# Two state-space layers on a 64x64 image: another load of x, a convolution shared three to one, and a table load moved behind two copies

## The chip, the cores and the metric

The kernel runs on one core of one Trainium2 chip. The metric is the device time of one execution in microseconds; the median of three runs stands for the kernel. The profile is of one further execution, with its own time. In the text, PE or TensorE is the matrix engine, DVE is VectorE, ACT is ScalarE, POOL is GpSimd, and SP is the engine that issues most of the transfers.

## What is computed

The input x is an image of 64x64 positions with 96 channels. Two layers of the same kind are applied, each added to its own input:

```python
x = x + _L0_conv_ref(_gn(x), ...)
x = x + _L1_conv_ref(_gn(x), ...)
```

`_gn` normalises the 96 channels in 32 groups of three, over all positions of a group. A layer then is, cut to what matters:

```python
xz = x @ in_proj_w                      # 96 -> 2 * 192
x_val, z = xz[..., :192], xz[..., 192:]
xc = conv3x3_depthwise(x_val) + conv_b
u = silu(xc)
y = sum of four selective scans over u  # rows and columns, both ways, 16 states each
y = layernorm(y) * ln_g + ln_b
y = y * silu(z)
return y @ out_proj_w
```

Layer 0 and layer 1 differ in the form of the scan and in the orders in which the positions are visited.

## The kernel before

**Layout.** Channels lie on partitions and the 4096 positions along the free axis. `xT` holds the 96 channels of x, 96x4096. The 192 inner channels are kept as three blocks b = 0, 1, 2 of 64 channels. A block has 128 partitions: partitions 0 to 63 hold its channels for one half of the positions and 64 to 127 those of the other half. Each half has four chunks c of 512 positions (eight image rows); `NCH` is 4 and `HT` 512. `u`, `y` are such blocks of 128x2048.

**Constants and the load of x** (lines 84 to 163). ScalarE loads the table for exponential and logarithm, VectorE and GpSimd build an identity, selectors and other constants, and `gav` (the matrix that averages groups of three channels, line 120) is read. Then x is read in eight pieces of 512 positions, alternately from the SP queue and the ScalarE queue, into tiles `xt` of which four exist. A partition receives four separate positions of 96 floats, 384 B each (line 158). TensorE transposes each piece in four products into a PSUM tile `pt`, and VectorE copies that into `xT` (line 163). At the end of the program text, but before the layers, VectorE takes `bn_stats` of each piece of `xT` (line 1347), and `xT` is stored to a buffer `xs` in DRAM (line 1348), from which the end of the layer reads it back.

**A layer.** The weights are read on the SP queue (lines 1353 to 1359 and `scan_weights`, lines 189 to 215); `ds` is a small sum over weights on VectorE (line 1361). Then come `head`, the scans, and `tail`.

**`head`** (from line 1123). Zero borders are set on three padded images `pad`. `bn_aggr` (line 1141) joins the statistics; two small products with `gav` give the mean `gm` and the variance of each group, and ScalarE makes `rs`, one over the deviation, from a logarithm and an exponential (lines 1150 and 1151). VectorE normalises `xT` into `xn` in eight pieces (line 1156). `project(b, c)` multiplies with the input weights and ScalarE copies the result into `pad` (lines 1163 and 1167); `borders(b)` computes the neighbouring rows once more for the chunk edges (lines 1181 and 1185). Then the 3x3 convolution runs in two forms:

- `conv(b, s)` on VectorE, two chunks at a time: nine taps on shifted views, one scaling (line 1237) and eight multiply-and-adds into `acc` (line 1239), of which three buffers exist.
- `conv_by_products(b, c)` on TensorE, one chunk: nine products with diagonal matrices `diag` (lines 1216 and 1251). A product in fp32 shows as two entries in the profile.

VectorE does blocks 0 and 1, TensorE block 2. `finish` (line 1206) applies Silu on ScalarE into `u`, and starts `y` as u times `ds` (line 1121). `gate(b, c)` projects z on TensorE (line 1193), applies Silu on ScalarE into `sz`, of which three buffers exist (line 1198), and stores that to `szd` (line 1199), twelve times.

**Scans.** Layer 0 runs `near_scans` (from line 246), a short form in which only states near the ends of the sequence matter, with a test; the full form `far_scans` runs only if the test fails. Layer 1 runs `scans` (from line 654), in eight groups of a direction and a chunk. There every instruction is kept behind the one before it on its engine in program text, with a list of due slots for the preparation of later groups. All its instructions show line 668, a helper. `first` prepares the first group: projections `pj` of the last chunk of all three blocks, their copies `xd`, the products `pd` and from them, per block, Abs, exponential and logarithms on ScalarE. ScalarE's table for exponential and logarithm is loaded ahead of all that; the head has used the table of Silu.

**What sets the order.** Outside `scans` a scheduler orders the instructions of each engine when the program is built: among instructions that it takes as ready it picks the one that stands first in the program text. Each engine then follows its own fixed order and waits at each instruction for its inputs and buffers. The memory of the load's tiles is used again by the head, and that of the head by the scans, so that the later part waits for the earlier one's last readers.

Of the kernel before, what the change touches and what calls it, by code (L numbers as in the profile page):

```python
# [8 lines left out]
F32 = mybir.dt.float32  # L9
BF16 = mybir.dt.bfloat16  # L10
AF = mybir.ActivationFunctionType
ALU = mybir.AluOpType
# [4 lines left out]
HW = 64  # L17
L = HW * HW
DM = 96
# [5 lines left out]
HT = TC // 2  # L25
NCH = L // TC
SR = HT // HW
# [16 lines left out]
def two_ss2d_layers(  # L44
# [41 lines left out]
    def load_exp_ln():  # L86
        table("natural_log_exp_and_others")
# [3 lines left out]
    ident = const.tile([128, 128], F32, name="ident")  # L91
# [25 lines left out]
    eps5 = const.tile([128, 1], F32, name="eps5")  # L117
    nc.vector.memset(eps5, 1e-5)
    gav = const.tile([DM, DM], F32, name="gav")
    nc.sync.dma_start(out=gav, in_=gavg)  # L120

# [25 lines left out]
    xs = dpool.tile([DM, L], F32, name="xs")  # L147
# [2 lines left out]

    xp = ExitStack()
    xT = xp.enter_context(tc.tile_pool(name="xT0", bufs=1)).tile([DM, L], F32, name="xT0")
    with tc.tile_pool(name="ld", bufs=4) as ld, tc.tile_pool(
        name="ldp", bufs=4, space=PSUM
    ) as ldp:
        xr = x.rearrange("(g j p) c -> g p j c", p=128, j=4)
        for g in range(8):
            xt = ld.tile([128, 4, DM], F32, tag="xt", name=f"xt{g}")
            (nc.sync if g % 2 == 0 else nc.scalar).dma_start(out=xt, in_=xr[g])
            pt = ldp.tile([DM, 512], F32, tag="pt", name=f"pt{g}")  # L160
            for j in range(4):
                nc.tensor.transpose(pt[:, j * 128 : (j + 1) * 128], xt[:, j, :], ident)
            nc.vector.tensor_copy(xT[:, g * 512 : (g + 1) * 512], pt)

    def columns(t, h, cols):

# [487 lines left out]
    def scans(weights):  # L654
# [4 lines left out]
        xw, dwb, _ = weights  # L659
# [13 lines left out]
        with ExitStack() as sc:  # L673
# [1 line left out]
            mn = sc.enter_context(tc.tile_pool(name="mn", bufs=3))  # L675
            pps = sc.enter_context(tc.tile_pool(name="pps", bufs=1, space=PSUM))
            dram = sc.enter_context(tc.tile_pool(name="dram", bufs=3, space=DRAM))
            load_exp_ln()
            am = []
            carry = pre.tile([128, 3, NP], F32, name="carry")  # L680
            PER = 3 * NP
# [234 lines left out]
            def first(  # L916
                project, projected, rows, delta, spread, tokens_B, tokens_B_out,
                first_part, less_part, next_part, tokens_du, tokens_du_out,
            ):
                parts = [delta(T) for T in range(3)]  # L920
                for h in range(2):
                    project(h)
                for h in range(2):
                    projected(h)
                rows()
                for begin, by_scalar, by_vector in parts:
                    begin()
                tokens_B()
                for T, (begin, by_scalar, by_vector) in enumerate(parts):
                    by_scalar()  # L930
                    if T == 1:
                        tokens_B_out()
                        am.extend(decays(weights[2]))
                    by_vector()
                    spread(T)
                    if T < 2:
                        fetch_c(0, T)
                stage_a(0)
                for h in range(2):
                    first_part(h)  # L940
                for h in range(2):
                    less_part(h)
                for h in range(2):
                    next_part(0, h)
                for h in range(2):
                    less_part(h)
                for e in range(4):
                    tokens_du(e)
                for e in (0, 2, 1, 3):
                    tokens_du_out(e)  # L950
                for h in range(2):
# [171 lines left out]
    def head(l, xT, w):  # L1123

        ipw_s, v, ds = w["ipw"], w["v"], w["ds"]
        with ExitStack() as sc:
            cv = sc.enter_context(tc.tile_pool(name=f"cv{l}", bufs=1))
            cw = sc.enter_context(tc.tile_pool(name=f"cw{l}", bufs=3))
# [7 lines left out]
                nc.gpsimd.memset(t[HALF[1], NCH - 1, SR + 1, 1 : HW + 1], 0.0)  # L1136


            gst = cv.tile([DM, 6], F32, name=f"gst{l}")
            gm, rs = gst[:, 2:3], gst[:, 5:6]  # L1140
            nc.vector.bn_aggr(gst[:, 0:2], w["st"].rearrange("p a b -> p (a b)"))
            pm = cvp.tile([DM, 1], F32, tag="z", name=f"pm{l}", bufs=3)
            nc.tensor.matmul(pm, gav, gst[:, 0:1], start=True, stop=True)
# [6 lines left out]
            nc.scalar.activation(rs, pv, AF.Ln, bias=eps5[0:DM])  # L1150
            nc.scalar.activation(rs, rs, AF.Exp, scale=-0.5)

            xn = cv.tile([DM, L], F32, name=f"xn{l}")
            for g in range(8):
                s = slice(g * 512, (g + 1) * 512)
                nc.vector.tensor_scalar(xn[:, s], xT[:, s], gm, rs, ALU.subtract, ALU.mult)
            xr = xn.rearrange("p (r w) -> p r w", w=HW)

            def project(b, c):
# [43 lines left out]
            W2 = HW + 2  # L1203

            def finish(b, cut, of):
                nc.scalar.activation(
                    u[b][:, cut].rearrange("p (c r w) -> p c r w", r=SR, w=HW), of, AF.Silu,
                    bias=v[:, b, V_CB : V_CB + 1],
                )
                start_y(nc.scalar.mul, ds, b, cut)  # L1210
# [14 lines left out]
            def conv(b, s):  # L1225


                room = cw.tile([128, 2, SR, W2], F32, tag="acc", name=f"acc{l}_{b}_{s}")
                acc = room.rearrange("p c r w -> p c (r w)")[:, :, 0 : SR * W2 - 2]
                for k, (i, j) in enumerate(taps):  # L1230
                    o = i * W2 + j
                    src = pad[b].rearrange("p c r w -> p c (r w)")[
                        :, 2 * s : 2 * s + 2, o : o + SR * W2 - 2
                    ]
                    wk = v[:, b, V_CW + k : V_CW + k + 1]
                    if k == 0:
                        nc.vector.tensor_scalar_mul(acc, src, wk)
                    else:
                        nc.vector.scalar_tensor_tensor(acc, src, wk, acc, ALU.mult, ALU.add)  # L1239
                finish(b, slice(1024 * s, 1024 * (s + 1)), room[:, :, :, 0:HW])  # L1240

            for b in (0, 1, 2):
                project(b, 0)
# [5 lines left out]
            diag = cv.tile([128, len(taps), 128], F32, name=f"diag{l}")  # L1249
            for k in range(len(taps)):  # L1250
                nc.scalar.mul(diag[:, k, :], ident, v[:, 2, V_CW + k : V_CW + k + 1])
            conv(0, 0)
            for c in range(NCH):
                conv_by_products(2, c)
            for b, s in ((1, 0), (0, 1), (1, 1)):
                conv(b, s)
            for b in range(3):
                for c in range(NCH):
                    gate(b, c)
# [82 lines left out]
                    if 0 <= i - lag < NCH:  # L1342
                        step(order[i - lag])

    st = [pers.tile([DM, 8, 6], F32, name=f"st{l}") for l in range(2)]
    for g in range(8):
        nc.vector.bn_stats(st[0][:, g, :], xT[:, g * 512 : (g + 1) * 512])
    nc.sync.dma_start(out=xs, in_=xT)
    for l in range(2):

        w = {"st": st[l], "next": st[1]}
# [16 lines left out]
        else:  # L1368
# [6 lines left out]
        xT = xp.enter_context(tc.tile_pool(name=f"xT{l + 1}", bufs=1)).tile(  # L1375
            [DM, L], F32, name=f"xT{l + 1}"
        )
# [81 lines left out]
```

## Time and profile before

| what | value |
|---|---|
| median of three runs | 1553.86 us (1553.56 to 1554.03) |
| profiled execution, its own time | 1545.96 us |
| its span in the profile | 1543.8 us |
| load of x and statistics, to the start of `xn` in layer 0 | 0 to 23.61 us |
| head of layer 0, to the first product of `near_scans` | 23.61 to 89.05 us |
| `near_scans` and the tail of layer 0, to the start of `xn` in layer 1 | 89.05 to 225.63 us |
| head of layer 1, to the first projection of `scans` | 225.63 to 289.95 us |
| granted TensorE clock, whole span | 0.913 of full speed |

In a line of a timeline the columns are: start in us from the start of the span, length in us, engine, line of the kernel, operation, output and input by the names of the tiles, shape, count of instructions that the line merges, and in brackets how long the engine stood idle before it and what released it. A line that merges several instructions gives the time from the first start to the last end. PEld is the loading of weights into TensorE; a name with q (SPq, ACTq) is an engine's queue, where transfers are issued. In the chain that ended last the columns are start, length and what the time was spent in.

### The profile page before, as it was taken

The numbers are of one execution on the slowest core, as the hardware profiler recorded it, in microseconds if no ns is written. First come the engines' busy times: TensorE is split into PE (matmuls) and PEld (weight loads), VectorE is DVE, ScalarE is ACT, GpSimd is POOL, SyncE is SP. The second block draws the span as 40 slices with busy tenths as digits, with TensorE's granted clock in tenths as the row PEclk, the third lists the DMA queues.
The fourth block names the chain that finished last, engine by engine and source line by source line (L and its number), as shares of the span: only waits on it lengthen the run. The fifth ranks groups of instructions, "written<-read, shape, count | busy, mean of one in ns | idle before, by whom it ended". The sixth has DMA issues, their size and how long they took to land.

```text
span 1543.8 us, 17370 instructions
## 1 busy us (share of the span) xinstructions
PE 1258.3 (82%) x5158; PEld 507.0 (33%) x5158; DVE 1354.3 (88%) x942; ACT 1196.7 (78%) x2459; POOL 1102.9 (71%) x593
## 2 busy tenths in 40 slices
PE   5953779798897888798888889797979888877778
PEld 3432424233332323232323333333333332322223
DVE  6936389469999999999999999999999999999976
ACT  3456125669989898898999999999898989897733
POOL 0032100149898999899898989898989899998860
PEclk8975689869999999998999999999999899999999
DMA  4031330441625344352626162526263544526223
GB/s 111 11 107 45 89 87 1 127 106 37 144 74 133 82 111 108 85 126 68 151 55 153 55 138 57 137 57 146 65 140 76 124 97 96 123 70 146 74 81 96
DMA packets 82674, 146.32 MB, mean 95 GB/s; under 512 B 31580, under 2 KB 33820, under 8 KB 82476
## 3 DMA queue, kind: packets, MB, share of 16 engines
q1 hardware_dynamic: 79884, 142.78, 38.2%
q0 software_dynamic: 576, 1.57, 0.4%
q10 hardware_dynamic: 2112, 0.79, 0.2%
q8 instruction: 42, 0.69, 0.2%
q14 instruction: 60, 0.49, 0.1%
HBM read 80.85 MB, written 12.13 MB: 60 GB/s over the span
## 4 chain that ended last, share of the span: by engine, by line
DVE 26%; issue 21%; PE 13%; ACT 11%; POOL 7%; DMA 6%; SPq 5%; DVEq 0%; POOLq 0%; ACTq 0%
DVE h L668 17%; DVE b L668 6%; POOL hc L668 5%; SPq L668 5%; ACT a L668 4%; PE ys L668 3%; ACT bT L668 2%; PE pj L668 2%; PE b L668 2%; PE cp L1216 2%; DMA cb<-C 2%; DMA du<-su 2%; DMA xT<-xs 1%; PE pd L668 1%; PE in L1163 1%
## 5 line engine op out<-in xcount | busy, mean ns | idle before, releaser
L668 POOL TENSOR_TENSOR hc<-h,cb 128x1024 f32<-128x1024 f32 x384 | 902.7, 2367 | 116.3 <-DVE h L668 61.8
L668 DVE TENSOR_TENSOR_SCAN h<-a,carry,b 128x1024 f32<-128x1024 f32 x288 | 665.2, 2337 | 30.3 <-PE b L668 6.4
L668 ACT ACTIVATE a<-dt,am 128x1024 f32<-128x1024 f32 x384 | 438.6, 1142 | 94.3 <-DVE h L668 91.3
L668 PE MATMUL ys<-hc,fold 128*64 128x512 f32 x1536 | 434.2, 645 | 2.6 <-POOL hc L668 2.6
L668 ACT ACTIVATE bT<-duT,BT 128x192 f32<-128x192 f32 x1012 | 387.2, 445 | 8.3 <-PE b L668 6.4
L668 PE MATMUL b<-ident,bT 128*128 128x128 f32 x1536 | 223.5, 289 | 34.3 <-DVE h L668 27.4
L668 DVE TENSOR_TENSOR b<-b,du 128x1024 f32<-128x1024 f32 x192 | 232.2, 1209 | 12.3 <-PE b L668 12.3
L668 PEld LDWEIGHTS b<-ident,bT 128*128 128x128 f32 x1536 | 176.6, 147 | 160.9 <-DVE h L668 99.1
L668 DVE TENSOR_TENSOR_SCAN h<-a,b 128x1024 f32<-128x1024 f32 x96 | 216.1, 2278 | 13.9 <-PE b L668 6.0
L668 PE MATMUL b<-B,selh 96*128 96x512 bf16 x384 | 122.4, 402 | 90.0 <-DVE h L668 89.9
L668 PEld LDWEIGHTS ys<-hc,fold 128*64 128x64 f32 x1536 | 79.0, 140 | 142.2 <-issue 102.8
L668 PEld LDWEIGHTS <-selh 96*128 96x128 bf16 x384 | 25.9, 98 | 220.9 <-DVE h L668 124.1
L668 PE MATMUL pj<-u,xw 64*124 64x512 f32 x192 | 94.2, 636 | 3.1 <-ACT sz L1198 1.7
L668 PE MATMUL pd<-xd,dwb 29*64 29x512 f32 x192 | 58.2, 677 | 47.0 <-DVE w L668 40.1
L1239 DVE SCALAR_TENSOR_TENSOR acc<-pad,v,acc 128x1052 f32<-128x1052 f32 x64 | 79.6, 1308 | 0.2
L668 POOL DMA_DIRECT2D du<-su x12 | 6.4, 538 | 81.7 <-ACT am L226 79.7
L668 PE MATMUL ys<-y,ident 128*128 128x512 f32 (+1 forms) x120 | 64.7, 646 | 0.0
L1216 PE MATMUL cp<-pad,diag 128*128 128x512 f32 x144 | 62.3, 593 | 0.0
L668 ACT CAST B<-pj 96x512 bf16<-96x512 f32 (+2 forms) x96 | 54.9, 575 | 4.5 <-PE pj L668 4.5
L668 POOL TENSOR_TENSOR sp<-sp,ln 128x512 f32<-128x512 f32 x45 | 57.4, 1275 | 0.2
L668 POOL TENSOR_TENSOR ln<-ln,w 128x512 f32<-128x512 f32 x45 | 57.4, 1276 | 0.0
L668 POOL TENSOR_TENSOR su<-sp,u 128x512 f32<-128x512 f32 x45 | 57.3, 1274 | 0.0
(173 smaller groups left out, 1173.7 us busy)
## 6 DMA issues: line engine op xcount, KB each, us to landing
cb<-C SPq DMA_DIRECT2D x256, 256.0 KB, 4.1
dt<-sp SPq DMA_DIRECT2D x192, 128.0 KB, 4.2
du<-su SPq DMA_DIRECT2D x180, 128.0 KB, 4.2
szd<-sz SPq DMA_DIRECT2D x24, 256.0 KB, 3.1
szt<-szd SPq DMA_DIRECT2D x24, 256.0 KB, 6.8
xT<-xs SPq DMA_DIRECT2D x8, 384.0 KB
xs<-xT SPq DMA_DIRECT2D x1, 1536.0 KB
xs<-xT SPq DMA_DIRECT2D x8, 192.0 KB, 2.3
```

The costliest lines, as they stand in the source:

```text
L668: return lambda *args, **more: tc.keep_in_program_order(op(*args, **more))
L1163: nc.tensor.matmul(ps[half], ipw_s[:, 64 * b : 64 * b + 64], xn[:, g * 512 : (g + 1) * 512], start=True, stop=True,)
L1216: nc.tensor.matmul(ps.rearrange("p (r w) -> p r w", w=HW), diag[:, k, :], pad[b][:, c, i : i + SR, j : j + HW], start=(k == 0), stop=(k == ...
L1239: nc.vector.scalar_tensor_tensor(acc, src, wk, acc, ALU.mult, ALU.add)
```

## The change

Six edits are made:

1. The load of x. A partition now receives four consecutive positions, 1536 B in one piece. All eight transfers are issued ahead of the transposes, into eight buffers. The copy from PSUM into `xT` is made by ScalarE and puts the positions in order, so that it writes every fourth element in turn. The statistics are taken by VectorE from PSUM, in the same loop.
2. The store of `xT` to `xs` and the read of `gav` stand at the end of the load, in this order; `st` is allocated ahead of it.
3. Normalisation: every second piece of `xn` is made by ScalarE as an Identity with scale `rs` and bias `shift`, which VectorE computes beforehand as minus mean times `rs`.
4. TensorE convolves chunks 0 to 2 of block 2; chunk 3 is convolved by VectorE, as the last of its convolutions. `conv` takes a range of chunks.
5. `load_exp_ln()` of `scans` stands behind the two copies `projected` of the first group, and no longer at the start.
6. In `gst` a seventh column holds `shift`.

```diff
-    nc.sync.dma_start(out=gav, in_=gavg)
...
-    with tc.tile_pool(name="ld", bufs=4) as ld, tc.tile_pool(
+    st = [pers.tile([DM, 8, 6], F32, name=f"st{l}") for l in range(2)]
+    with tc.tile_pool(name="ld", bufs=8) as ld, tc.tile_pool(
         name="ldp", bufs=4, space=PSUM
     ) as ldp:
-        xr = x.rearrange("(g j p) c -> g p j c", p=128, j=4)
+        xr = x.rearrange("(g p j) c -> g p j c", p=128, j=4)
+        xts = [ld.tile([128, 4, DM], F32, tag="xt", name=f"xt{g}") for g in range(8)]
         for g in range(8):
-            xt = ld.tile([128, 4, DM], F32, tag="xt", name=f"xt{g}")
-            (nc.sync if g % 2 == 0 else nc.scalar).dma_start(out=xt, in_=xr[g])
-            pt = ldp.tile([DM, 512], F32, tag="pt", name=f"pt{g}")
+            (nc.sync if g % 2 == 0 else nc.scalar).dma_start(out=xts[g], in_=xr[g])
+        for g in range(8):
+            pt = ldp.tile([DM, 4, 128], F32, tag="pt", name=f"pt{g}")
             for j in range(4):
-                nc.tensor.transpose(pt[:, j * 128 : (j + 1) * 128], xt[:, j, :], ident)
-            nc.vector.tensor_copy(xT[:, g * 512 : (g + 1) * 512], pt)
+                nc.tensor.transpose(pt[:, j], xts[g][:, j, :], ident)
+            nc.scalar.copy(
+                xT[:, g * 512 : (g + 1) * 512].rearrange("c (p j) -> c j p", j=4), pt
+            )
+            nc.vector.bn_stats(st[0][:, g, :], pt.rearrange("c j p -> c (j p)"))
+    nc.sync.dma_start(out=xs, in_=xT)
+    nc.sync.dma_start(out=gav, in_=gavg)
...
-            load_exp_ln()
             am = []
...
                 for h in range(2):
                     projected(h)
+                load_exp_ln()
                 rows()
...
+            nc.vector.scalar_tensor_tensor(shift, gm, -1.0, rs, ALU.mult, ALU.mult)
...
-                nc.vector.tensor_scalar(xn[:, s], xT[:, s], gm, rs, ALU.subtract, ALU.mult)
+                if g % 2 == 0:
+                    nc.vector.tensor_scalar(xn[:, s], xT[:, s], gm, rs, ALU.subtract, ALU.mult)
+                else:
+                    nc.scalar.activation(xn[:, s], xT[:, s], AF.Identity, bias=shift, scale=rs)
...
-            conv(0, 0)
-            for c in range(NCH):
+            conv(0, slice(0, 2))
+            for c in range(NCH - 1):
                 conv_by_products(2, c)
-            for b, s in ((1, 0), (0, 1), (1, 1)):
-                conv(b, s)
+            for b, c in ((1, 0), (0, 2), (1, 2)):
+                conv(b, slice(c, c + 2))
+            conv(2, slice(NCH - 1, NCH))
...
-    st = [pers.tile([DM, 8, 6], F32, name=f"st{l}") for l in range(2)]
-    for g in range(8):
-        nc.vector.bn_stats(st[0][:, g, :], xT[:, g * 512 : (g + 1) * 512])
-    nc.sync.dma_start(out=xs, in_=xT)
```

More of the change, by code (lines that the diff above doesn't have):

```diff
@@ L1136, in head @@
                 nc.gpsimd.memset(t[HALF[1], NCH - 1, SR + 1, 1 : HW + 1], 0.0)
-            gst = cv.tile([DM, 6], F32, name=f"gst{l}")
-            gm, rs = gst[:, 2:3], gst[:, 5:6]
+            gst = cv.tile([DM, 7], F32, name=f"gst{l}")
+            gm, rs, shift = gst[:, 2:3], gst[:, 5:6], gst[:, 6:7]
             nc.vector.bn_aggr(gst[:, 0:2], w["st"].rearrange("p a b -> p (a b)"))
@@ L1225, in conv @@
             def conv(b, s):
-                room = cw.tile([128, 2, SR, W2], F32, tag="acc", name=f"acc{l}_{b}_{s}")
+                n = s.stop - s.start
+                room = cw.tile([128, 2, SR, W2], F32, tag="acc", name=f"acc{l}_{b}_{s.start}")
+                room = room[:, 0:n]
                 acc = room.rearrange("p c r w -> p c (r w)")[:, :, 0 : SR * W2 - 2]
@@ L1232, in conv @@
                     src = pad[b].rearrange("p c r w -> p c (r w)")[
-                        :, 2 * s : 2 * s + 2, o : o + SR * W2 - 2
+                        :, s, o : o + SR * W2 - 2
                     ]
@@ L1239, in conv @@
                         nc.vector.scalar_tensor_tensor(acc, src, wk, acc, ALU.mult, ALU.add)
-                finish(b, slice(1024 * s, 1024 * (s + 1)), room[:, :, :, 0:HW])
+                finish(b, slice(HT * s.start, HT * s.stop), room[:, :, :, 0:HW])
             for b in (0, 1, 2):
```

## The prediction

> **What bounds the kernel now.** I read the busy shares and the slices first, then the chain that ended last, then the timelines of VectorE, TensorE and ScalarE over the two places that the change touches: the load of x (0 to 24 us) and the two heads (24 to 89 us and 226 to 290 us). The page says that VectorE leads, and that the chain is spread over all engines:
>
> ```profile
> PE 1258.3 (82%) x5158; PEld 507.0 (33%) x5158; DVE 1354.3 (88%) x942; ACT 1196.7 (78%) x2459; POOL 1102.9 (71%) x593
> ...
> DVE 26%; issue 21%; PE 13%; ACT 11%; POOL 7%; DMA 6%; SPq 5%; DVEq 0%; POOLq 0%; ACTq 0%
> ```
>
> The 88% come from the second layer's scans (about 290 to 1494 us), which the change leaves alone but for one table load. So the whole-kernel shares say nothing here; the stages must be read alone. VectorE in the load (columns: start, us, engine, line, operation, out<-in):
>
> ```profile
> 6.42 0.17 DVE L1361 TENSOR_REDUCE ds<-v 128x3 f32<-128x12 f32 x1 [3.49 <-DMA v<-in_vec_dram]
> ...
> 9.16 2.47 DVE L163 COPY xT<-pt 96x512 f32<-96x512 f32 x4
> ...
> 15.91 0.69 DVE L163 COPY xT<-pt 96x512 f32<-96x512 f32 x1 [0.17 <-PE pt L162]
> 16.51 4.24 DVE L1347 BATCH_NORM_STATS2 st<-xT 96x6 f32<-96x512 f32 x7
> 20.79 0.37 DVE L1141 BATCH_NORM_AGGREGATE gst<-st 96x2 f32<-96x48 f32 x1
> ```
>
> The reader sees one engine do copies and statistics in turn, after standing 3.49 us in front of a reduction of a late weight. TensorE transposed the first four groups at 4.49 to 8.11 us and had to wait for buffers until 12.22. The aggregate at 20.79 starts everything else: normalisation begins 2.82 us later, at 23.61.
>
> The end of the first head, from ScalarE's timeline and the whole timeline:
>
> ```profile
> 74.26 0.69 ACT L1206 ACTIVATE u<-cp,v 128x512 f32<-128x512 f32 x1 [1.17 <-PE cp L1216]
> 75.28 0.60 ACT L1198 ACTIVATE sz<-z 128x512 f32<-128x512 f32 x1 [0.33 <-PE z L1193]
> ...
> 84.85 1.84 ACT L1198 ACTIVATE sz<-z 128x512 f32<-128x512 f32 x3 [2.05 <-DMA szd<-sz]
> 87.70 1.30 ACT L1198 ACTIVATE sz<-z 128x512 f32<-128x512 f32 x2 [1.01 <-DMA szd<-sz]
> ...
> 89.05 0.30 PEld L276 LDWEIGHTS nu<-u,wide 128*128 128x128 f32 x2 [2.50 <-ACT sz L1198]
> ```
>
> and the chain of waits through the second head:
>
> ```profile
> 245.69 31.10 PE cp L1216 x72
> 276.79 1.02 PE z L1193 x3
> ...
> 283.08 2.47 DMA szd<-sz
> ...
> 286.82 2.38 DMA szd<-sz
> ...
> 289.95 3.80 PE pj L668 x12
> ```
>
> The order is: convolution of block 2 on TensorE, then all twelve gates (z, Silu, store), then the scans. VectorE's last tap ends at 71.98+2.67 = 74.65 in layer 0 and at 259.72+17.48 = 277.20 in layer 1, 12.7 and 14.4 us before the head is over. TensorE's convolution and then the gates are the path; VectorE has slack.
>
> **What the Trainium skill says.** "TensorE: Matmul & The Clock Gate", Part 4: PE-mode transpose, says that transposes do not count as work that releases the engine's clock gate. The trace agrees in effect: 16 transposes took 3.62 us in both bursts, 0.226 us each, no faster at the end of a burst. I therefore price 32 in a row at the same rate. "ScalarE: Activation LUTs", What ACT_TABLE_LOAD costs, gives about 1283 ns for a table load and about 93 ns for each per-partition pointer operand; the trace has 1.28 us for each load, and 0.72 us for a 128x512 ScalarE product with one pointer (y<-u,ds), so a normalisation with two is an estimated 0.8 us from these. "SBUF — State Buffer", Door 1: The DMA port swizzle, warns that accesses which leave a 16-byte line each time are slower; the new copies write every fourth float. No row of this trace shows such a write. "DMA: Bandwidth & Descriptors", Specifications, asks for pieces of at least 512 B; x was read in pieces of 384 B and becomes 1536 B. But the trace moved 296 GB/s at 4.4 to 5.4 us with the small ones, so I credit nothing for it beyond an earlier start.
>
> **The change part by part.**
>
> *Load.* Removed from VectorE: eight copies (5.2 us busy). The statistics read PSUM instead of xT, eight at their present spacing of 0.61 us. ScalarE, idle from 2 to 15.96 us, takes the copies: a comparable ScalarE eviction (pad<-in, 128x512) is 0.59 us, so about 0.5 to 0.6 us each; if the strided write doubles it, 1.2 us. With eight input buffers no load waits for one. On SP's queue the four x loads, 0.4 us of issue each, now go back to back; gav, ipw and v come after them. gav stands behind the xs store in the program, but it waits for nothing and the scheduler may issue it while the store waits; it is needed only when the statistics end. TensorE then transposes 32 in a row: from about 4.3 us, 32 x 0.226 = 7.24, to 11.6. ScalarE (8 x 0.6) and VectorE (8 x 0.61) keep pace with 0.9 us per group. The last statistics end about 0.8 us later: 12.4, a gain of 8.4. The other end: v's issue slips by 0.7 us (two more x loads in front), and it shares the rings with twice the x data; if it lands at 7 to 8.4 and VectorE again stands before the ds reduction, the constants behind it (6.42 to 9.16, 2.74 us) and the eight statistics (4.9) end at 14.6 to 16.0, a gain of only 4.8 to 6.2. Doubled copies give 5+8x1.2 = 14.6 for ScalarE, inside the same end. I take 7.5. The nine diag products (2.74 us on ScalarE) and the pad memsets wait for the end of the transposes as now and stay beside the 2.82 us chain of small steps; at worst they delay the Ln by 1 us, within these ends. The xs store moves up with the copies and nothing waits for it soon.
>
> *Normalisation, twice.* A [96,1] product (0.19 us of spacing as its neighbours L1145 to L1147) is put ahead of the first piece: +0.2 each time. Four pieces go to ScalarE at 0.7 to 0.8 us, ready about 3.1 us in, against 3.73 for all eight on VectorE. The first pad copy came 3.06 us in (26.67 against 23.61), bound by TensorE at a clock of 0.64 in that stage, so I book no gain: +0.4 for both. Bounds -0.8 (TensorE slots that one early gate took in layer 1) to +0.8.
>
> *Convolution.* TensorE loses one chunk of block 2: nine taps of two passes, 72 passes in 31.10 us, so 18 x 0.432 = 7.8 us. VectorE gains the same chunk: its taps on 128x1052 follow at 14.78/12 = 1.23 us, of which 1.10 is the length (1052 elements) at one per 0.96 GHz cycle, a rate that the normalised g rows (512 elements, 0.66 us apart) bear out; half the length is 0.68 us. Eight of these and a first tap of about 0.4: 5.8 us. There are three acc buffers, and the older convolutions have precedence, so the short one fills in behind and ends last.
>
> Head of layer 0, counted from the start of normalisation (23.61): TensorE's convolution ended at 50.5, now 42.7; first gate at 43.9; twelve gates took 13.7 us (75.28 to 89.00), in layer 1 12.1, so they end at 56.0 to 57.6. VectorE ended at 51.0, now 56.8; the last Silu (0.69) gives 57.5. Before, the end was at 65.4. Ideal gain 7.8. I take off 0.8, because ScalarE's order is fixed at build time: before, u<-acc of block 1 ran at 76.86 although its data were there at 74.65. So -7.0. Head of layer 1, from 225.63: gates end at 269.0+1.1+12.1 = 282.2; VectorE 283.0, last Silu 283.7, against 289.95 for the first projection of the scans, which does need chunk 3 of block 2 first. That is -6.2, less 1.0 for the same order: -5.2. What is late next in both heads is the last Silu of block 2, with the gates' stores a microsecond before it.
>
> *Table load.* Now at 289.92, under the projection (3.80 us), at no cost. ScalarE's copies came at 292.87 and 293.79 and the first Abs at 295.53, waiting for PE. Moved behind the copies, it runs from 294.4 to 295.7: +0.15. Its other bound is +1.28, if the projection through dwb were to come earlier.
>
> Sum: -7.5 + 0.4 - 7.0 - 5.2 + 0.15 = -19.15. The span goes from 1543.8 to about 1524.6; the profiled execution, 1545.96 with 2.16 around its span, to 1526.8. The median of the runs is 7.90 above the profiled execution; I keep that distance: 1553.86 - 19.15 = 1534.7.
>
> **Rivals.**
>
> (A) *Half the gain.* VectorE stands before ds again (-5), and ScalarE runs a finished block's y products and Silus ahead of gates, so that each head gains 3. For it: the 3.49 us wait above, and the order at 76.86. Against: nothing on ScalarE is full in this stage (37.2 of 89 us). -5 - 6 + 0.5: 1543.4.
>
> (B) *The heads give nothing.* The stores of sz (4.1 us to landing in layer 0, three buffers) or the later last Silu take all that the products leave, and only the load's 7.5 stays: 1546.4. Against: between 60 and 74 us the DMA engines were idle, so gates that start then meet no other traffic.
>
> (C) *Slower: the gates stay behind the last convolution.* If ScalarE's fixed order sets both last Silus and their y products (0.69+0.72+1.15+1.15 = 3.7 us) ahead of the gates, a head ends at 56.8+3.7+12.9 = 73.4 from its start, against 65.4 and 64.3: +8.0 and +9.1. With the load's -7.5: +9.6, 1563.5. It decides once a head ends over 3.5 us later than now (half of the load's gain, less normalisation): with k gates behind, 56.8+3.7+1.08k over 68.4, so from the eighth gate. For it: ScalarE put the fourth product's Silu before the first gate at 74.26. Against: there the Silu was ready a microsecond before the gate; now twelve gates are ready 13 us before it.
>
> **How the numbers follow.** Forecast 0.67, own range 1529 to 1541; A 0.13; B 0.08; C 0.12. The forecast's best end is -8.4 and both ideal heads (-14.0) with -0.8 from normalisation, -23.2: 1530.7, and I give it 2 us for what a shifted schedule does in the first layer's scans. A and B lie within 1528 to 1547, which leaves out C and little else. A measurement of this kernel tells about 0.2% (3.1 us) from none. Faster: forecast, A, most of B, 0.86; same 0.03; slower 0.11.
>
> **What would show it.** In the changed profile: the aggregate near 13 us instead of 20.79; ScalarE copies of xT spaced as the transposes; 54 passes of cp per layer, and z starting some 43 us after normalisation; the last acc tap about 57 us after it with u Silu just behind; nu and pj released by that Silu or by a gate within a microsecond or two; the table load between the second xd copy and Abs. Wrong would be: statistics after 15 us, gates on ScalarE behind the last acc, or a scan stage of layer 1 (pj to the last scan) longer than now by more than a microsecond.

## The result and the profile after

Median 1529.9 us (1526.23 to 1532.2, four runs) against 1553.71 us (1544.35 to 1554.03) for the kernel before beside it: a ratio of 0.9866, 95% interval 0.9838 to 0.9893. Run again later, 1533.01 us against 1549.71: 0.9895, 0.9874 to 0.9916. The forecast of 1534.7 us (0.9877 of 1553.86) lies inside both intervals, but the forecast of the profiled execution, 1526.8 us, was 3.7 below the 1530.49 measured. The profiled execution has a span of 1528.7 us, 15.1 less than before. Its stages say that the forecast is not right term by term:

| stage | before, us | after, us | change | forecast |
|---|---|---|---|---|
| load, to the first `xn` | 23.61 | 20.46 | -3.15 | -7.5 |
| head 0, first `xn` to the first product of `near_scans` | 65.45 | 56.44 | -9.01 | -6.8 |
| `near_scans` and tail 0 | 136.57 | 134.97 | -1.60 | 0 |
| head 1, first `xn` to the start of `pj` | 64.32 | 56.56 | -7.76 | -5.0 |
| start of `pj` to the first Abs | 5.58 | 10.75 | +5.17 | +0.15 |
| first Abs to the last scan | 1198.00 | 1197.07 | -0.93 | 0 |
| last scan to the end | 50.27 | 52.45 | +2.18 | 0 |

The forecast's column puts half of the 0.4 for normalisation into each head. The changes add up to -15.1. The last two rows are in code that none of the edits touches; over all runs below the scans took 1194 to 1206 us (e3 apart) and the tail 50.1 to 53.7. So spans and medians move by several microseconds from run to run for reasons outside the change, and I judge parts by their stage.

The page's busy line, and its shares of the chain:

```profile
PE 1238.4 (81%) x5122; PEld 499.9 (33%) x5122; DVE 1358.4 (89%) x946; ACT 1209.9 (79%) x2475; POOL 1103.3 (72%) x593
...
DVE 27%; issue 22%; PE 15%; ACT 10%; POOL 5%; DMA 5%; SPq 4%; DVEq 0%; ACTq 0%; POOLq 0%
```

They tell as little as before: VectorE has 4 us more, TensorE 20 us less. The load tells more. VectorE's timeline:

```profile
8.40 0.17 DVE L1372 TENSOR_REDUCE ds<-v 128x3 f32<-128x12 f32 x1 [5.46 <-DMA v<-in_vec_dram]
...
11.15 2.48 DVE L168 BATCH_NORM_STATS2 st<-pt 96x6 f32<-96x512 f32 x4
14.11 0.69 DVE L168 BATCH_NORM_STATS2 st<-pt 96x6 f32<-96x512 f32 x1 [0.48 <-ACT xT L165]
...
17.56 0.37 DVE L1148 BATCH_NORM_AGGREGATE gst<-st 96x2 f32<-96x48 f32 x1
```

TensorE's timeline, and ScalarE's:

```profile
6.45 1.94 PE L164 MATMUL pt<-ident,xt 128*96 128x128 f32 x8 [0.56 <-DMA xt<-in_x_dram]
11.89 3.65 PE L164 MATMUL pt<-ident,xt 128*96 128x128 f32 x16 [3.50 <-DVE st L168]
```

```profile
5.08 1.98 ACT L165 COPY xT<-pt 96x512 f32<-96x512 f32 x2 [3.06 <-PE pt L164]
...
13.02 3.78 ACT L165 COPY xT<-pt 96x512 f32<-96x512 f32 x4 [3.47 <-PE pt L164]
```

VectorE still stands before `ds`, now 5.46 us. The statistics that lie behind it hold all four PSUM buffers, so TensorE stands 3.50 us too, released by a statistic (st). The copies come about 0.9 us apart (3.78 for four), where an eviction of this size was priced at 0.6; one alone takes 1.06 to 1.12 us, since each begins before the one ahead of it has ended. From 14.11 on each statistic is released by a copy.

Why `v` is late stands in the timeline of SP's queue, first before, then after, and in SP's waits (in all, times, longest, in us):

```profile
2.74 1.37 SPq L1357 DMA_DIRECT2D v<-in_vec_dram  x2
```

```profile
5.33 1.38 SPq L1368 DMA_DIRECT2D v<-in_vec_dram  x2
...
SPq L1368 <- DMA ipw<-in_ipw_dram: 1.1, 1, 1.1
```

`v` is issued 2.6 us later than before, and by the profile its issue waited 1.1 us for the transfer of `ipw`.

The end of head 0, on VectorE and on ScalarE:

```profile
70.78 0.49 DVE L1251 TENSOR_SCALAR acc<-pad,v 128x526 f32<-128x526 f32 x1
...
73.21 5.65 DVE L1253 SCALAR_TENSOR_TENSOR acc<-pad,v,acc 128x526 f32<-128x526 f32 x7
```

```profile
63.70 1.13 ACT L1210 ACTIVATE sz<-z 128x512 f32<-128x512 f32 x2
...
76.25 0.60 ACT L1210 ACTIVATE sz<-z 128x512 f32<-128x512 f32 x1
78.89 0.72 ACT L1218 ACTIVATE u<-acc,v 128x512 f32<-128x512 f32 x1 [2.04 <-DVE acc L1253]
```

The twelve gates (sz) go through beside VectorE's taps, from 63.70 to 76.85; the first product of `near_scans` starts at 76.90. The last Silu of block 2 comes at 78.89, and that product did not wait for it. In head 1 the chain of waits and ScalarE's timeline show what did wait:

```profile
230.22 23.39 PE cp L1228 x54
...
268.43 8.07 PE pj L675 x12
276.50 2.65 PE pd L675 x4
```

```profile
270.18 0.72 ACT L1218 ACTIVATE u<-acc,v 128x512 f32<-128x512 f32 x1 [1.80 <-DVE acc L1253]
...
276.54 0.59 ACT L675 COPY xd<-pj 124x512 f32<-124x512 f32 x1 [2.50 <-PE pj L675]
277.14 1.28 ACT L84 ACT_TABLE_LOAD   x1
279.18 0.60 ACT L675 ACTIVATE wl<-pd 128x512 f32<-128x512 f32 x1 [0.75 <-PE pd L675]
```

TensorE's 72 passes in 31.10 us have become 54 in 23.39. `pj` starts 7.8 us earlier, counted from the first `xn`, but takes 8.07 us instead of 3.80. It reads `u` of block 2, which is there at 270.90, and its passes are slow. TensorE's timeline and the busy times by window (window, its length, busy us of PE, PEld, DVE, ACT and POOL with counts, granted TensorE clock, DMA share, GB/s), first before, then after:

```profile
289.95 3.80 PE L668 MATMUL pj<-u,xw 64*124 64x512 f32 x12 [1.69 <-ACT sz L1198]
...
289.90:293.80 3.90, 3.85 (x13) 1.82 (x14) 0.00 (x0) 1.88 (x4) 0.00 (x0) 1.00 0.36 134
```

```profile
268.43 8.07 PE L675 MATMUL pj<-u,xw 64*124 64x512 f32 x12 [3.49 <-ACT sz L1210]
...
271.00:276.50 5.50, 5.50 (x10) 2.17 (x10) 0.38 (x1) 1.24 (x2) 0.00 (x0) 0.50 0.00 0
```

The granted clock is 0.50 where it was 1.00, and most passes last 1.05 us instead of 0.59. The first Abs then waits for `pd`, with the table load already done.

### The profile page after: what moved, and what is told of

Read it like the earlier page. It is cut to its first block, busy times and chain, and to the rows that moved or that the text cites. A ratio compares the mean times of both kernels' runs of the same rounds, so it can differ in the third digit from the quotient of the medians.

```text
span 1528.7 us, 17324 instructions
## 1 busy us (share of the span) xinstructions
PE 1238.4 (81%) x5122; PEld 499.9 (33%) x5122; DVE 1358.4 (89%) x946; ACT 1209.9 (79%) x2475; POOL 1103.3 (72%) x593
## 4 chain that ended last, share of the span: by engine, by line
DVE 27%; issue 22%; PE 15%; ACT 10%; POOL 5%; DMA 5%; SPq 4%; DVEq 0%; ACTq 0%; POOLq 0%
DVE h L675 17%; DVE b L675 7%; PE ys L675 4%; ACT a L675 4%; SPq L675 4%; POOL hc L675 4%; PE b L675 3%; PE pj L675 3%; DMA cb<-C 2%; ACT bT L675 2%; PE pd L675 2%; PE cp L1228 2%; DMA szt<-szd 1%; DVE w L675 1%; PE in L1175 1%
## 5 line engine op out<-in xcount | busy, mean ns | idle before, releaser
L675 PE MATMUL b<-ident,bT 128*128 128x128 f32 x1536 | 219.5, 287 | 33.9 <-DVE h L675 28.3
L675 PE MATMUL pj<-u,xw 64*124 64x512 f32 x192 | 98.4, 662 | 4.8 <-ACT sz L1210 3.5
L1253 DVE SCALAR_TENSOR_TENSOR acc<-pad,v,acc 128x1052 f32<-128x1052 f32 (+1 forms) x80 | 91.3, 1198 | 0.7
L675 POOL TENSOR_TENSOR sp<-sp,ln 128x512 f32<-128x512 f32 x45 | 57.6, 1279 | 0.2
L675 POOL TENSOR_TENSOR ln<-ln,w 128x512 f32<-128x512 f32 x45 | 57.6, 1280 | 0.0
L675 PEld LDWEIGHTS pj<-u,xw 64*124 64x124 f32 x192 | 35.2, 198 | 65.0 <-issue 45.5
```

The source lines that it names most:

```text
L675: return lambda *args, **more: tc.keep_in_program_order(op(*args, **more))
```

## The experiments

Each is the changed kernel but for the edit shown. Times in one stage are counted from the first `xn` of that layer.

**Load undone (e1).** Edits 1 and 2 are taken back to the load of before.

```diff
-        xr = x.rearrange("(g p j) c -> g p j c", p=128, j=4)
...
-            nc.scalar.copy(
...
-            nc.vector.bn_stats(st[0][:, g, :], pt.rearrange("c j p -> c (j p)"))
+            nc.vector.tensor_copy(xT[:, g * 512 : (g + 1) * 512], pt)
...
+    for g in range(8):
+        nc.vector.bn_stats(st[0][:, g, :], xT[:, g * 512 : (g + 1) * 512])
```

> The changed kernel with the load of x, the copies, the statistics and the read of gav as before; split convolution, shared normalisation and table load stay. If the load is worth what the two profiles show (normalisation of layer 0 starts at 20.46 instead of 23.61 us), it starts at 23.6 again, the heads keep their lengths of the changed kernel (56.4 us to the first product of near_scans, 67.3 us from normalisation to the first Abs of layer 1), and the span is 3.2 us longer than 1528.7. If the heads owe their gain to the earlier load or to its quieter transfers, they go back towards 65.4 and 69.9 us and the span is 10 us or more longer.

The first `xn` came at 23.12 us, the heads took 56.64 and 67.69 (to Abs) against 56.44 and 67.31. Median 1536.53 us, ratio to the kernel before 0.9915 (0.9886 to 0.9943). In these profiles the new load is worth 2.7 to 3.2 us, and the heads owe it nothing.

**All of block 2 on TensorE (e2).** The split is undone, the rest stays.

```diff
-            for c in range(NCH - 1):
+            for c in range(NCH):
                 conv_by_products(2, c)
...
-            conv(2, slice(NCH - 1, NCH))
```

> The changed kernel with all four chunks of block 2 on TensorE. If the split makes the heads' gain: first product of near_scans 65 us after normalisation (56.4 with the split), last acc tap 6 us earlier, projection of layer 1 in under 4 us, first Abs 69 to 70 us after normalisation (67.3 with the split); span +11 us. If shared normalisation or the shifted schedule makes a part of it, the heads come out 1 us or more shorter than the 65.4 and 69.9 of the kernel before.

Head 0 took 66.67 us, head 1 71.09 to Abs: 10.2 and 3.8 us longer than in the changed kernel. Median 1550.71 us, ratio 0.9988 (0.9966 to 1.0009). Its chain of waits:

```profile
240.42 31.12 PE cp L1228 x72
...
287.64 3.81 PE pj L675 x12
```

`pj` is back at its short length, because block 2 is finished before the gates again. TensorE stood 1.06 us ahead of it, and its passes ran at a granted clock of 1.00. So the split makes the heads' gain, and also the longer `pj`. From the start of `pj` to Abs it is 5.73 us here, 5.58 before: with a short `pj` the table load behind the copies costs 0.15.

**`ds` behind the statistics (e4).** The reduction is fixed at its place in program text, after the load.

```diff
-        nc.vector.reduce_sum(ds, v[:, :, V_D : V_D + 4], axis=AX.X)
+        tc.keep_in_program_order(
+            nc.vector.reduce_sum(ds, v[:, :, V_D : V_D + 4], axis=AX.X)
+        )
```

> The changed kernel, but the small sum ds is kept behind the statistics on VectorE, so that the constants no longer wait for the weight v. If that wait cost what the load missed: constants done by 6 us, transposes without the gap of 3.5 us, statistics end near 13.5 us at the pace of the ScalarE copies (0.93 us each), normalisation at 16.5 us instead of 20.46, span -4 us. If the copies or the transfers of x bind anyway, normalisation stays at 19.5 us or later.

First `xn` at 16.89 us, 3.57 earlier; median 1526.86 us, ratio 0.9837 (0.9816 to 0.9859). VectorE's timeline:

```profile
4.42 1.29 DVE L128 CAST selh<-i 96x1024 bf16<-96x1024 f32 x2
6.07 0.69 DVE L168 BATCH_NORM_STATS2 st<-pt 96x6 f32<-96x512 f32 x1 [0.35 <-ACT xT L165]
...
13.41 0.69 DVE L168 BATCH_NORM_STATS2 st<-pt 96x6 f32<-96x512 f32 x1 [0.21 <-ACT xT L165]
```

The constants are done at 5.7 instead of 11.2. Now every statistic starts 0.03 us after the end of the copy of its tile, eight times, though it needs only the transposes (the 0.2 us in brackets is how long VectorE stood idle): two readers of one PSUM tile ran one after the other. In the changed kernel's last four groups it is the same.

**Statistics ahead of the copies (e5)**, on top of e4: the `bn_stats` line is put ahead of the copy.

> The run with ds behind the statistics, and in addition the statistics written ahead of the ScalarE copy for each piece. There every statistic started 0.2 us after the end of the copy of the same PSUM tile. If the two readers of one tile are kept one behind the other in the order of the text, now the statistics start with the end of the transposes and the copies wait: aggregate at 13.1 to 13.4 us instead of 14.14, and copies end about 1 us later. If they only followed the transposes, nothing moves (14.1).

The order turned round. The aggregate was early, 12.90 us, but the copies ended at 15.4, and TensorE's product for the mean, released by the last copy, came only at 15.48. First `xn` at 18.11, 1.2 later than in e4. The aggregate alone is not the milestone. A single run took 1524.81 us, with a scan stage of 1194.4 us that has nothing to do with it.

**Copies written in line (e6)**, on top of e4: the old layout, so that ScalarE writes neighbouring floats and x is read in 384 B pieces again.

```diff
-        xr = x.rearrange("(g p j) c -> g p j c", p=128, j=4)
+        xr = x.rearrange("(g j p) c -> g p j c", p=128, j=4)
...
-                xT[:, g * 512 : (g + 1) * 512].rearrange("c (p j) -> c j p", j=4), pt
+                xT[:, g * 512 : (g + 1) * 512].rearrange("c (j p) -> c j p", j=4), pt
```

> The run with ds behind the statistics, but x read in pieces of 384 B in the old order of positions, and the copies written in line. If the write of every fourth element makes the copy slow, it takes 0.55 to 0.6 us instead of 0.98, and the aggregate comes 0.4 us earlier, as the transposes (0.89 us for a group) then set the pace; if the copy is slow because it reads PSUM beside VectorE, it stays near 0.98. The smaller pieces should lower the 330 to 390 GB/s of the load towards the 314 of the kernel before.

ScalarE's timeline:

```profile
8.95 0.58 ACT L165 COPY xT<-pt 96x512 f32<-96x512 f32 x1 [0.27 <-PE pt L164]
```

A copy takes 0.58 us (in e4 1.07 to 1.11) and waits for TensorE. First `xn` at 15.07 us, 1.82 ahead of e4. The copies explain only a part of this. From the end of the last transpose to the end of the last statistic it is 1.5 us instead of 2.1. Another 0.5 us comes from x: TensorE's second row of transposes starts at 6.12 instead of 6.65, although from 3.5 to 7 us the small pieces moved 311 GB/s and the large ones of e4 338. And 0.6 us comes from that row itself, 24 transposes in 4.71 us instead of 5.35, because the last of them ran faster. So the larger pieces, with the scattered writes that they bring, cost this load more than they gave; what the order of the writes is worth alone, no run separates. A single run: 1526.39 us.

**Block 2 last in `pj` (e7).** Its passes go behind those of blocks 0 and 1 of both halves.

```diff
-                for h in range(2):
-                    project(h)
+                for Ts in ((0, 1), (2,)):
+                    for h in range(2):
+                        project(h, Ts)
```

> The changed kernel, but the first group's projections run blocks 0 and 1 for both halves first and block 2 last, so that 4 passes instead of 8 are left when the last Silu of block 2 arrives. If the projection of 8.07 us is long because it stands in front of block 2 and then runs on at a low clock, the first Abs comes 2 to 3 us earlier after normalisation (64.5 to 65.3 us instead of 67.3), span -2 to -3 us. If the passes left after the wait do not matter, because the clock is low in any case and the last copy sets the end, under 1 us.

`pj` took 5.20 us, the first Abs came 64.90 us after `xn` instead of 67.31. ScalarE's timeline:

```profile
276.85 1.07 ACT L675 COPY xd<-pj 124x512 f32<-124x512 f32 x2 [2.03 <-PE pj L675]
277.94 1.28 ACT L84 ACT_TABLE_LOAD   x1
279.24 0.60 ACT L675 ACTIVATE wl<-pd 128x512 f32<-128x512 f32 x1
```

Four passes instead of eight need the last Silu, and 2.4 us of the lost gain come back, though the granted clock over `pj` was 0.55. Here Abs directly follows the table load. The median, 1529.86 us (ratio 0.9853, 0.9826 to 0.988), shows none of it beside e4's 1526.86 or the changed kernel's. In the profiled execution, the slowest of the four with 1537.06 us, the scan stage was 1205.7 us long.

**The table load at its old place (e3).** `load_exp_ln()` goes back to the start of `scans`.

> The changed kernel with the table load at the start of the scans again. In the changed kernel Abs came 0.75 us after the load, waiting for TensorE; so if that wait is the rule, the first Abs stays 67.3 us after normalisation, within the half microsecond or so by which TensorE's clock moves it. If the load stands on the path behind the copies, Abs comes up to 1.3 us earlier after the second xd copy (1.2 us or less between copy end and Abs, now 2.05).

A miss. A single run took 1603.48 us, 73 more in the span. ScalarE's timeline and its groups by line:

```profile
270.98 1.28 ACT L84 ACT_TABLE_LOAD   x1
272.26 1.28 ACT L1218 ACT_TABLE_LOAD   x1
273.56 0.72 ACT L1218 ACTIVATE u<-acc,v 128x512 f32<-128x512 f32 x1
...
283.18 1.28 ACT L675 ACT_TABLE_LOAD   x1
284.47 0.63 ACT L675 ACTIVATE wl<-wl 128x512 f32<-128x512 f32 x1
...
285.86 1.28 ACT L675 ACT_TABLE_LOAD   x1
287.16 0.72 ACT L675 ACTIVATE wl<-wl,one 128x512 f32<-128x512 f32 x1
```

```profile
L675 ACT ACT_TABLE_LOAD x96 | 123.2, 1283 | 1.5
```

The load now ran ahead of the last Silu of block 2, whose table was then loaded over it. From there on the shared table was gone: a table was loaded ahead of the exponential (`wl<-wl`) and another ahead of the logarithm (`wl<-wl,one`), 96 loads in all, and the scans grew from 1197.07 to 1266.20 us. A later load is no refinement of the change; with the last Silu so late, it has to stand behind it.

**Normalisation on VectorE alone (e8)**: `if g % 2 == 0` becomes `if g >= 0`.

> The changed kernel with all eight pieces of the normalisation on VectorE (the shift is still computed). With the shared normalisation the first acc tap came 9.4 to 9.5 us after its start against 8.4 and 9.0 before, and TensorE took twelve passes before the first border. If sharing changes that order and delays VectorE's convolution, the first tap comes back to 8.4 to 9.0 and the heads get 0.5 to 1 us shorter at the last Silu of block 2 (58.3 us after normalisation in layer 1). If it does not matter: 9.4 again, or later by the 1 us that the last pieces of xn take longer.

Heads of 56.68 and 67.13 us (to Abs) against 56.44 and 67.31. Normalisation took 3.7 us instead of 3.0, the first tap came 1.0 us earlier in layer 0 and 0.3 later in layer 1. Sharing it is worth nothing net that can be seen here. A single run: 1539.12 us, with a scan stage of 1205.0.

**The three useful edits together (e9)**: e4, e6 and e7.

> Three edits together: ds pinned behind the statistics, ScalarE's copies written in line (384-byte pieces again), block 2's passes last in both halves of pj. If the gains add, the first normalised piece starts at 15.1 us (5.4 below the changed kernel), the product pj takes about 5.2 us and the first Abs stands 64.9 us after layer 1's first normalised piece (67.3 in the changed kernel): 7.8 us less in all before the scans, a median near 1522 us. The rival, that each gives back what the other brings: pj waits for the same last Silu anyway, Abs stays at 65.6 as with the in-line copies alone, and the median is 1524 to 1527 us. A scan stage of other length (1194 to 1206 us in the runs so far) is told apart by the stage times.

1521.49 us (1520.78 to 1525.8, five runs), ratio 0.9825 (0.9803 to 0.9848), with the changed kernel at 1533.01 us on the same chip: faster than both. First `xn` at 13.68 us, `pj` 4.61 long, first Abs 63.20 us behind `xn`. The load beat the expectation of 15.1 through TensorE. Its timeline, and its transposes in the windows of 3 to 7 and 7 to 8 us (columns: minimum, median and maximum duration in ns, first and last start):

```profile
3.73 5.67 PE L164 MATMUL pt<-ident,xt 128*96 128x128 f32 x32 [3.73 <-DMA xt<-in_x_dram]
```

```profile
L164 PE MATMUL pt<-ident,xt x16: 421/421/422, 3.7 to 6.9; 128*96 128x128 f32 x16
...
L164 PE MATMUL pt<-ident,xt x9: 272/273/421, 6.7 to 7.9; 128*96 128x128 f32 x9
```

This time no piece of x was late; about 3.5 us into an unbroken row of transposes they became faster, from 421 to 273 ns, and followed each other after 0.11 instead of 0.21 us.

**The table load at the start of `scans`, behind a late Silu (e10)**, on top of e9: the short convolution is traced behind the gates, so that the last ScalarE instruction ahead of `scans` is block 2's `y`.

```diff
-            conv(2, slice(NCH - 1, NCH))
             for b in range(3):
                 for c in range(NCH):
                     gate(b, c)
+            conv(2, slice(NCH - 1, NCH))
...
+            load_exp_ln()
             am = []
...
-                load_exp_ln()
                 rows()
```

> As the run with three edits, and the last quarter's convolution traced behind the gates, with the table load back at the start of the scans: now the load has to stand behind the last Silu and y of block 2 and before the copies of xd. Theory (the load was harmful there only because the last traced ScalarE instruction was a gate): no further table loads appear in the scans, their stage stays within 1194 to 1206 us, and the first Abs follows the second copy of xd or the product pd, 0.3 to 1.2 us earlier than in the run with three edits; a median of about 1521 us. Rival (a load at the start of the scans is harmful wherever it lands): the scans grow to about 1266 us again and the time to about 1595 us.

```profile
265.64 0.72 ACT L1131 ACTIVATE y<-u,ds 128x512 f32<-128x512 f32 x1
266.38 1.28 ACT L84 ACT_TABLE_LOAD   x1
268.29 1.07 ACT L675 COPY xd<-pj 124x512 f32<-124x512 f32 x2 [0.63 <-issue]
270.52 0.60 ACT L675 ACTIVATE wl<-pd 128x512 f32<-128x512 f32 x1 [1.16 <-PE pd L675]
```

In this timeline of ScalarE the load lies in idle time, no table is loaded in the scans (1198.5 us), and the theory of e3 holds. But Abs gained next to nothing: it stands 1.16 us behind the second copy, waiting for `pd`, where e9 with the load between had 1.31. Median 1521.53 us, the same as e9. The move that hides the load wins 0.15 us.

**The changed kernel again (e11).**

> The changed kernel as it is, beside the others on one chip: a median of 1527 to 1533 us, the first normalised piece at 20.5 us, the first Abs 67.3 us after layer 1's. If it comes out as fast as the two versions, their gain before the scans is lost later.

1533.01 us; first `xn` at 20.52, first Abs 67.31 us behind `xn` in layer 1. The stages of one and the same program repeat within 0.1 us in these two profiles. Programs that share a stage differ by more. With the load of the changed kernel the first `xn` came at 20.46 to 21.73 us (e2, e3, e7 and e8 have it too), and with its heads and `pj` the first Abs came 65.57 to 67.69 us after `xn` (e1, e4, e5 and e6). So a difference of 1 or 2 us between two experiments counts only where the trace also shows its cause. For the load it does: in all six profiles the first `xn` stands 11.9 to 12.1 us behind the start of `ds`, which moved from 8.40 to 9.83 with the landing of `v`.

## Why the prediction was right, and where not

*The total was right, partly by cancellation.* The two heads with normalisation and table load were put at -11.65 us and measured -11.60 (-9.01 and -2.59 to Abs), but head 0 was 2.2 us too small and head 1 2.3 too large. The load was 4.35 us too large. Undisturbed by the change, the other stages added -0.35 in the profiled pair. The forecast's sum of -19.15 thus stands against -15.1 in the spans, -23.8 in the first medians and -16.7 in the second. There is luck in the median too: the forecast kept the 7.90 us by which the median of the kernel before stood above its profiled execution, and for the changed kernel it stood 0.59 below. One reading of the prediction is the wrong way round: the end of VectorE's taps lay 14.4 us ahead of the head's end in layer 0 and 12.7 in layer 1. No sum uses it.

*Load: the term that failed.* The step chose 7.5 between a good end of 8.4 and a bad one of 4.8 to 6.2. The bad one came and went beyond: 3.15. Its sign was named, statistics after 15 us: the aggregate started at 17.56. Three things were missing. First, the step let the issue of `v` slip by 0.7 us, with `gav` and `ipw` behind all four x loads of SP's queue. It slipped by 2.6 us; `gav` and `ipw` went out between the first and the second x load, and by the profile `v` waited for `ipw` to land. So `ds` came at 8.40, the late end of the guess, and VectorE did stand before it. Second, waiting statistics hold the PSUM buffers and so stop TensorE, 3.50 us; the step let TensorE run on to 11.6 while VectorE waited. e4 puts the wait for `v`, with all that it held up, at 3.57 us. Third, the scattered copies came 0.90 to 0.91 us apart in a row, not 0.5 to 0.6, and the statistics were held behind them, while the step ran both side by side. The other end, 1.2, was on record, but only as ScalarE's own sum, with no one behind it. With the wait and the scattered writes out of the way the first `xn` comes at 15.07 (e6), 8.5 us before that of the kernel before. That this meets the good end of 8.4 is partly chance: there the statistics still ran behind the copies, x was late once, and some transposes were faster than the 0.226 us that the step used.

The Trainium skill, "SBUF — State Buffer", Door 1: The DMA port swizzle, had warned of the scattered writes, and the runs agree with its direction: a copy took 1.06 to 1.12 us against 0.58. For transposes the step leaned on the Trainium skill's "TensorE: Matmul & The Clock Gate", Part 4: PE-mode transpose, that they don't release the clock gate. The changed kernel's bursts, 16 in 3.65 us, agree; e9 does not, where later transposes took 273 ns, nor do the ends of rows in e1, e2, e3, e5, e6, e8 and e10. There the measurement decides: a row of transposes alone can become faster.

*Normalisation: right, at about nothing.* Forecast +0.4, bounds 0.8 either way; e8 differs from the changed kernel by +0.24 and -0.18 us in the heads. A piece on ScalarE took 0.80 us, as estimated.

*Convolution: mechanism right.* TensorE's 54 passes took 23.39 us, 7.7 less (forecast 7.8). VectorE's taps ran 48.9 us instead of 42.6, +6.3 for +5.8; the last ended at 58.40 for 56.8 predicted, of which about 1 us is a later first tap (9.50 against 8.41). The gates ended at 56.39, inside 56.0 to 57.6. In head 0 the step made the last Silu of block 2 the end; the runs show the gates as the end: the scans' first product starts at 56.44, and the Silu ends 2.7 us later (79.61 against 76.90) without being waited for. That is the 2.2 us of extra gain, against 58.6 in the forecast; the deduction of 0.8 in it was not needed. About half a microsecond of it was paid back in the next stage: from the first product of the scans to their next kind of product (`npj`) it took 7.78 us instead of 7.27.

In head 1 the step did see that the projection needs chunk 3 of block 2, and its Silu ended at 59.03 against 58.07. But it then carried the projection along at its old length. Two things made it longer. Eight of its twelve passes stood behind the Silu, so that the six passes of the second half started 2.62 us after the first pass of `pj`, where it had been 0.97: +1.65. And the granted clock fell to 0.50, so that these six took 5.45 us instead of 2.83, and the way from there to Abs 2.68 instead of 1.78: +3.5. Together these are the 5.17 of the table. The step asked when `pj` can start, and not how much of it remains behind its latest input, nor at what clock that runs; by these figures the clock is the larger part. e7 cuts the remainder and gets 2.4 us back. The clock went with the pause of TensorE ahead of `pj`: in the eleven profiles where it stood 2.55 to 3.50 us, most passes lasted 1.0 us or more, and in the two where it stood 1.06 and 1.69 us (e2 and the kernel before), all lasted 0.59 to 0.69. No experiment changes that pause alone, so it is not shown to be the cause. In e4 and e6 the passes came back to 0.59 us before the end of `pj`, which took 6.4 to 6.5 us, and Abs came 1.6 to 1.7 us earlier than in the changed kernel, with the same heads.

*Table load: the cost right, the reason missed.* In the changed kernel it is hidden (Abs waited 0.75 us longer for `pd`), and where `pj` is short it costs 0.15, as forecast, in e2 and between e9 and e10. What wasn't seen is that without this edit the split ends 73 us slower in the span (e3, a single run). Had the diff left the load where it was, my forecast would have been the same, and far wrong.

*Rivals.* A had the cause of the smaller load right and came nearer its size (5 against 3.15), but the heads did not halve. B is excluded by e2, C by the gates that ran beside VectorE's taps. e9 shows what the change left: 9.5 us in the spans (1519.2 against 1528.7), 11.5 in the medians on one chip.

What stays open: why the scans differ by up to 11 us between programs whose scans are the same; what takes the clock down ahead of `pj` and brings it back; and when transposes become faster. In e4 24 without a visible break in 5.35 us stayed at 417 ns, while in e1, e2, e3 and e8 the end of a row of 16 already fell to 273. None of this was tried.

## What to carry to other kernels

A tile that two engines read is freed by the later of them: before a statistic is moved from SBUF to PSUM, ask what stands ahead of it on its engine, since its wait then stops the producer. When a block's input becomes the latest, count the work that stands behind it, not only the start of what needs it, and put that input's share last. Look at the granted clock of that remainder too: a pause that a change opens ahead of it may be followed by slower passes. An instruction that changes state for all that follow on its engine, like a table load, has to be checked against every user of the old state whenever one of them moves.

## What the runs showed of the hardware

- Two readers of one PSUM tile, ScalarE's copy and VectorE's statistic, did not overlap in these programs: in e4 each statistic started 0.03 us after the end of the copy, and in e5, with the statistic first in the program text, the first copy started 0.03 us after the end of the first statistic (6.36 us, against 4.97 in e4).
- ScalarE's copy of 96x512 floats from PSUM took 0.58 us written in line (e6) and 1.06 to 1.12 us written to every fourth float (changed kernel), 1.8 to 1.9 times as long.
- fp32 transposes of 128x96 took 421 ns each and started 0.21 us apart, then 273 ns and 0.11 us apart, about 3.5 us into an unbroken row in e9. In seven other runs this came 2.2 to 4.1 us into a row; in e4 it did not come in a row of 5.35 us.
- The granted TensorE clock over `pj` was 1.00 after a pause of 1.06 us (e2) or 1.69 us (before), with passes of 0.59 us. In the changed kernel, after a pause of 3.49 us, it fell to 0.50, with passes of 1.05 us.
- After one table load ahead of a late Silu, 96 further loads of 1283 ns appeared in the scans (e3): 123.2 us of ScalarE's time, 69 us of the scan stage.
- SP's queue issued `v` at 5.33 us in the changed kernel, after a wait of 1.1 us for the transfer of `ipw`, as the profile infers it. In e2 and e3, with the same load, that wait was 2.3 and 2.9 us, and `ds` came at 9.49 and 9.83 us instead of 8.40.
